# GNN message passing with a segment maximum: the edge table spread by exclusive-or and float minimum

## The chip, the cores and the metric

One core of one Trainium2 chip runs the whole program. The metric is device microseconds (us) from launch to end of that program; lower is better. A core has five engines with instruction streams of their own: TensorE (PE in the profile, with its weight loads as PEld), VectorE (DVE), ScalarE (ACT), GpSimd (POOL) and SyncE (SP). In this kernel SP only issues transfers, and GpSimd issues the indirect ones, which gather rows by a list of indices. What an engine waits for is told to it by semaphores.

## The reference

One layer of a graph network over N = 6,250 nodes with D = 256 values each and E = 100,000 edges, which come sorted by their target `dst`:

```python
def reference(x, src, dst, theta_w, theta_b, phi_w, phi_b):
    x_src, x_dst = x[src], x[dst]
    e = relu((x_dst - x_src) @ theta_w.T + theta_b + x_src @ phi_w.T + phi_b)
    out = segment_max(e, dst, num_segments=N)
    out = where(isfinite(out), out, 0.0)
    return layernorm(x + out, axis=-1)          # over D, eps 1e-5
```

All values are float32. Since the maximum over the edges of a node commutes with adding what belongs to that node alone, what has to be computed per node is max over its edges of `b_rows[src]`, where `b_rows = x @ (phi_w - theta_w).T` is one table of 6,250 rows. The term of the target, the bias, the relu, the sum with x and the normalisation come at the end, once for each node.

## The kernel before, in words

**The table of rows.** x is read in 12 transfers (`x_q`), transposed on PE, copied by ACT and multiplied with the weights (L758); the result goes to `b_rows` in DRAM. The weights are the difference of the two given matrices, transposed on PE and copied by DVE (L739).

**Part 1, the first 1,130 nodes.** Their edges lie in 128 partitions of 146 columns. GpSimd gathers one column of 128 rows at a time (L512, one instruction for each column; `gather`), into a ring of six tiles `g` of eight columns. The first 48 columns are gathered from x itself and multiplied on PE; behind each of these gathers two instructions on a small tile (L488, `pause`) space them out. The other 98 columns come from `b_rows`. DVE folds a column into the running maximum of its partition (L688 in `run`, 146 of them, "steps"), SP stores eight steps at once (L696, `maxima`), and at the end one row per node is fetched back.

**Part 2, the other 5,120 nodes,** 40 tiles of 128. Here the edges are found on the chip. Each partition owns 40 nodes and looks at a window of 800 edges (`dst_w` and `src_w`, gathered from DRAM, L653). `fill_table` (L928 to L985) spreads them into a table of 36 ranks for each of 40 nodes (1,440 words in a partition): an edge's word is its distance to its place in the table times `WORD`, plus a code of its source, and ten steps move a word by 512, 256, ... 1 where its distance is at least that. A step is three DVE operations (L966, L969, L972), which go between two tables in turn. An empty place is a zero. At the end `padded` holds the codes as int16 by [rank, node], with a large code where there is no edge (L979).

A code says in which "slot" a source lies: b_rows is cut into 17 slots of 383 rows, three blocks of 128 with one row to spare, and the code is slot times 512 plus the row in the slot. `choice` (L995 to L1021) picks, for two slots at a time, at most one edge for each node and slot, by an exclusive-or of `padded` and a minimum over 24 ranks; `wanted` (L1023 to L1030) transposes the result `chosen` on PE and stores it as rows of words (`chosen_rows`). Then 85 "parts" follow, one for each slot and 1,024 nodes (`slot_part`, L1060): SP loads the words to all partitions (`want`, L1065), ACT makes a one-hot matrix from them in two operations for a block (L1071, L1072; from the list stage's end on, DVE makes one block of three, L1069), and PE multiplies it with the slot's rows, in two terms of reduced precision (L1057 by ACT, L1058 by DVE, from `raw`): 24 matmuls (L1079). DVE folds the result into `acc` (L1090; for slot 0 ACT copies it). `raw` is one tile for all slots. Its spare row needs a very small number, which a memset (L1034) puts there once; SP loads the rest for each slot.

**The list.** Edges that no slot took go to a list (`list_pieces`, L1171 to L1240): DVE marks and counts them, closes the gaps in 11 steps, and stores the words; 232 gathers from `b_rows` (`list_src`) follow, with running maxima of their own (again L688).

**The order.** Each engine's order is fixed when the program is built, by a scheduler that goes by the engines' modelled times and by who needs what; where an order is wanted it is written as a dependence without a semaphore (`behind_in_order`). So is GpSimd's (`in_turn`), and a step of part 1 behind the gathers of the next group. The top of the part around the change is

```python
fill_table()
paced[0] = 0
for s0 in range(0, NS, BATCH_S):
    choice(s0)
    wanted(s0)
    next_group_1(1)     # eight gathers, eight steps of the group before, one slot_part
```

and behind it come `list_pieces` and the rest of part 1, with two parts to a group, then the list's groups with the other parts, then the end: x + relu(...), the sums for the normalisation, and four stores. If an edge list doesn't fit the assumptions (counted in `bad`), a general path at the very end does the work anew; it is not taken here.

Of the kernel before, what the change touches and what calls it, by code (L numbers as in the profile page):

```python
# [41 lines left out]
I32 = mybir.dt.int32  # L42
# [5 lines left out]
ALU = mybir.AluOpType  # L48
# [4 lines left out]
P = 128  # L53
# [8 lines left out]
WINDOW = 800  # L62
R = 36
ROWS = 127
KB = 3
SLOT = 512
# [2 lines left out]
PAUSE = 160  # L69
CHOICE_R = 24  # L70
X_AFTER = 6
WORD = 8720
TABLE_BITS = 10
SLOT_BITS = 9
P_BITS = 7
# [3 lines left out]
OWN_LIST = 288  # L79
LIST_CHUNK = 232  # L80
LIST_GROUPS = (LIST + STEPS - 1) // STEPS
BACK = 34
# [3 lines left out]
FAR = 1000000.0  # L86
GENERAL_STEPS = 17
LOWEST = -1.0e30
ABSENT = 1 << 14
MAGIC = 12582912.0  # L90
PARTS = 2

# [335 lines left out]
def gnn_kernel(ctx: ExitStack, tc: tile.TileContext, x, src, dst, theta_w, theta_b, phi_w, phi_b, out):  # L428
    nc = tc.nc
    N, D = x.shape  # L430
# [9 lines left out]
    TR = TILES * R  # L440
    SLOT_ROWS = (KB - 1) * P + ROWS
    NS = -(-N // SLOT_ROWS)
    CW = 1024
    CHUNKS = OWN // CW
    EDGES = 1 << SORT_BITS
    NONE_1 = P * T1
    assert D == 2 * P and LEFT1 > 0 and OWN % CW == 0 and TILES < 64 and P * T1 < E and WINDOW < E
    assert (P - 1) * T + 1 < E <= P * T and N < ID_MASK and P * T <= EDGES and E + 8 * P <= EDGES
    assert SLOT * NS < min(ABSENT, WORD) and WORD << TABLE_BITS <= 1 << 24 and SLOT == 1 << SLOT_BITS and P == 1 << P_BITS and SLOT_ROWS < SLOT and KB == 3 and ROWS == P - 1 and WINDOW <= 8 * P and OWN_LIST * P < 1 << 20
    BATCH_S = 2  # L450
    assert STEPS == 1 << STEPS_BITS and LIST <= 2 * P and 3 * BATCH_S * CHOICE_R * TILES // 2 + TR <= 6 * WINDOW and LIST_CHUNK + 1 == LIST and LIST_CHUNK % STEPS == 0 and 3 * (BACK + LIST_CHUNK) <= WINDOW and BACK == R - 2 and CARRY_GROUPS * STEPS >= BACK and BACK + LIST_CHUNK <= OWN_LIST and R == 36 and CHOICE_R == 24 and OWN_LIST <= 512 and 1024 + OWN_LIST <= TR < 1024 + 512

# [34 lines left out]
    def iota(t, step, base, per_partition):  # L487
        return nc.gpsimd.iota(  # L488
            t,
            pattern=[[step, t.shape[1]]],  # L490
            base=base,
            channel_multiplier=per_partition,
            allow_small_or_imprecise_dtypes=True,
        )
# [7 lines left out]
    def behind_in_order(one, name, reason):  # L502
        after = mybir.DependencyInfo(mybir.DependencyClass.NoSync, mybir.DependencyReason.DATA)
        tc.add_manual_dep(one.ins, name, after, reason=reason)
# [80 lines left out]
    first_node = const.tile([P, 1], FP, name="first_node")  # L585
# [336 lines left out]
    def floor_of(to, value, divisor):  # L922
        nc.vector.tensor_scalar(
            to, value, 1.0 / divisor, -(divisor - 1) / (2.0 * divisor), op0=ALU.mult, op1=ALU.add
        )
        nc.vector.tensor_scalar(to, to, MAGIC, MAGIC, op0=ALU.add, op1=ALU.subtract)

    def fill_table():  # L928


        W = WINDOW
        local, w_1, w_2 = (wide[:, i * W : (i + 1) * W] for i in range(3))
        source, w_3 = work_2[:, :W], work_1[:, TR - W :]
        iota(w_3, 1, TR - W + 1, 0)
        nc.vector.memset(words[:, : TR - W], 0.0)
        nc.vector.memset(work_1[:, : TR - W], 0.0)
        nc.vector.tensor_scalar(local, dst_w, first_node, None, op0=ALU.subtract)

        nc.vector.tensor_scalar(bad[:, 1:2], local[:, 0:1], 0.0, None, op0=ALU.is_ge)
        far = W - (TR - (1 << TABLE_BITS)) - 1  # L940
        nc.vector.tensor_scalar(bad[:, 4:5], local[:, far : far + 1], 0.0, None, op0=ALU.is_lt)
        valid = w_1
        nc.vector.tensor_scalar(valid, local, 0.0, None, op0=ALU.is_ge)
        same = w_2
        nc.vector.memset(same[:, 0:1], 0.0)
        nc.vector.tensor_tensor(same[:, 1:], local[:, 1:], local[:, : W - 1], op=ALU.is_equal)
        nc.vector.tensor_tensor_scan(same, same, valid, 0.0, ALU.mult, ALU.add)
        nc.vector.tensor_scalar(
            source, same, float(R), None, op0=ALU.is_gt, op1=ALU.add, accum_out=bad[:, 5:6]
        )  # L950
        nc.vector.scalar_tensor_tensor(w_3, local, float(-R), w_3, op0=ALU.mult, op1=ALU.add)
        distance = w_3
        nc.vector.tensor_tensor(distance, w_3, same, op=ALU.subtract)
        nc.vector.tensor_copy(source, src_w)
        slot = local
        floor_of(slot, source, SLOT_ROWS)
        nc.vector.tensor_scalar(source, source, 1.0, None, op0=ALU.add)
        nc.vector.scalar_tensor_tensor(source, slot, float(SLOT - SLOT_ROWS), source, op0=ALU.mult, op1=ALU.add)
        nc.vector.scalar_tensor_tensor(source, distance, float(WORD), source, op0=ALU.mult, op1=ALU.add)
        nc.vector.tensor_tensor(words[:, TR - W :], source, valid, op=ALU.mult)  # L960
        now, then, going = words, work_1, work_2
        for i in reversed(range(TABLE_BITS)):
            step = 1 << i
            first = TR - W if step >= TR - W - step else 0
            a = max(first, step)
            nc.vector.tensor_scalar(  # L966
                going[:, a:], now[:, a:], float(-step * WORD), 0.0, op0=ALU.add, op1=ALU.max
            )
            nc.vector.scalar_tensor_tensor(  # L969
                then[:, first:], now[:, first:], float(step * WORD), now[:, first:], op0=ALU.is_lt, op1=ALU.mult  # L970
            )
            nc.vector.tensor_tensor(  # L972
                then[:, a - step : TR - step], then[:, a - step : TR - step], going[:, a:], op=ALU.add
            )
            now, then = then, now
        assert now is words
        nc.vector.tensor_scalar(work_1, words, 0.0, ABSENT + 1.0, op0=ALU.is_equal, op1=ALU.mult)
        nc.vector.scalar_tensor_tensor(
            padded.rearrange(by_rank, r=R),  # L979
            words.rearrange("p (j r) -> p r j", r=R),  # L980
            -1.0,
            work_1.rearrange("p (j r) -> p r j", r=R),
            op0=ALU.add,
            op1=ALU.add,
        )  # L985

# [44 lines left out]


    raw = slots.tile([P, KB, D], FP, name="raw", bufs=1)
    nc.vector.memset(raw, LOWEST)  # L1034
    terms_of = {}
    dve_hots = [0]

# [132 lines left out]

    def list_pieces():  # L1171
        left_over = wide_i16(3 * BATCH_S * CHOICE_R * TILES // 2, [P, TR])
        nc.vector.scalar_tensor_tensor(left_over, padded, float(ABSENT), unused, op0=ALU.is_lt, op1=ALU.mult)
        valid, count = work_1, work_2
        nc.vector.tensor_copy(valid.rearrange(by_node, r=R), left_over.rearrange("p (r j) -> p j r", r=R))
        nc.vector.tensor_tensor_scan(count, valid, valid, 0.0, ALU.add, ALU.max)  # L1176
# [15 lines left out]
            op=ALU.add,  # L1192
# [31 lines left out]
        for i, to in enumerate((second, third)):  # L1224
            nc.vector.tensor_scalar(mask, edge, ends[:, i + 1 : i + 2], None, op0=ALU.is_ge)
            nc.vector.copy_predicated(list_edges, mask, to)
        key, slot = (t.bitcast(I32)[:, :LIST_CHUNK] for t in (wide[:, WINDOW : 2 * WINDOW], count))
        nc.vector.tensor_scalar(key, list_edges[:, BACK:], (1 << 14) - 1, None, op0=ALU.bitwise_and)
        nc.vector.tensor_scalar(key, key, -1, 0, op0=ALU.add, op1=ALU.max)
        nc.vector.tensor_scalar(slot, key, SLOT_BITS, None, op0=ALU.logical_shift_right)  # L1230
        nc.vector.scalar_tensor_tensor(list_src, slot, SLOT_ROWS - SLOT, key, op0=ALU.mult, op1=ALU.add)
        nc.vector.tensor_scalar(list_src, list_src, N - 1, None, op0=ALU.min)
        list_node = list_edges
        nc.vector.tensor_scalar(list_node, list_edges, 14, (1 << 13) - 1, op0=ALU.logical_shift_right, op1=ALU.bitwise_and)
# [262 lines left out]
```

## Time and profile before

| | |
|---|---|
| median of 3 runs | 744.11 us (743.1 to 745.2) |
| the profiled execution's own time | 744.23 us |
| its span (first to last instruction) | 742.4 us |
| PE busy | 655.6 us, 88% of the span |
| DVE busy | 636.6 us, 86% |
| POOL busy | 515.8 us, 69% |
| ACT busy | 507.7 us, 68% |
| bytes moved | 164.83 MB, a mean of 222 GB/s |
| mean clock granted to TensorE | 0.969 of full speed |
| L1079 on PE, the parts' matmuls | 463.6 us in 1,960 recorded instructions, 397 ns each |
| L512 on POOL, gathers of part 1 from b_rows | 130.4 us in 98, 1,330 ns each |
| L688 on DVE, running maxima of both kinds | 180.3 us in 376, 479 ns each |

Busy times are shares of one profiled execution. Matmuls are pipelined, so a busy PE need not be at its peak. A "q" behind an engine's name (SPq, POOLq) marks its transfers. The chain that ended last is by lines 45% L1079; by engines PE 49%, DVE 8%, POOL 7%, DMA 6%, ACT 6%.

### The profile page before, as it was taken

To read this page: it belongs to the slowest core of one execution; us is meant where nothing else is said; L and a number is where in the kernel's file an instruction comes from. 1 tells how busy PE (TensorE), PEld (TensorE's weight loads), DVE (VectorE), ACT (ScalarE), POOL (GpSimd) and SP (SyncE) were. 2 spreads that over 40 slices of the span, in tenths; PEclk is the share of its full clock that TensorE was granted. 3 is DMA by queue.
4 is the path that set the end of the run, shared out by engine and by line. 5 is a ranking of instruction groups with operands and counts; after the bars stand their busy time and mean duration, and the time that the engine had idled before them with its cause. 6 is when DMAs were issued, how large, how long until landed. Compare 5 with 4: busy or idle time off the path is not lost.

```text
span 742.4 us, 10003 instructions
## 1 busy us (share of the span) xinstructions
PE 655.6 (88%) x3018; PEld 540.4 (73%) x3018; DVE 636.6 (86%) x1213; ACT 507.7 (68%) x714; POOL 515.8 (69%) x561
## 2 busy tenths in 40 slices
PE   0599998998875998899999999999999999789943
PEld 0388787886664866688888888888888888579943
DVE  6499999999987988498979888889888989968874
ACT  0144446969995797688778777877877776037882
POOL 7598987888987777777777777777767364037710
PEclk9999999999997899999999999999999999999986
DMA  7476756576477678988787878778867676336652
GB/s 219 135 254 207 274 192 221 167 255 205 139 228 231 215 215 300 300 295 271 235 264 221 283 250 248 242 240 284 269 209 244 186 255 208 137 107 192 206 200 76
DMA packets 56470, 164.83 MB, mean 222 GB/s; under 512 B 11899, under 2 KB 19860, under 8 KB 49332
## 3 DMA queue, kind: packets, MB, share of 16 engines
q1 hardware_dynamic: 32920, 98.76, 38.5%
q0 software_dynamic: 20944, 57.62, 27.3%
q10 hardware_dynamic: 2540, 7.69, 2.8%
q8 instruction: 27, 0.44, 0.3%
q14 instruction: 39, 0.32, 0.1%
HBM read 101.08 MB, written 63.74 MB: 222 GB/s over the span
## 4 chain that ended last, share of the span: by engine, by line
PE 49%; DVE 8%; POOL 7%; DMA 6%; ACT 6%; issue 4%; SPq 0%; DVEq 0%; ACTq 0%; POOLq 0%
PE ps_f L1079 45%; POOL g L512 6%; DMA g<-b_rows,src 4%; DMA want<-chosen_rows 2%; ACT x_f L1348 2%; ACT squares L1333 2%; PE ps_e L1303 2%; DVE acc L1090 2%; DVE g L688 1%; ACT x_t L1298 1%; DVE g L1314 1%; DVE x_f L1318 1%; PE ps_e L1296 1%; DVE work L1176 0%; POOL dst_w L512 0%
## 5 line engine op out<-in xcount | busy, mean ns | idle before, releaser
L1079 PE MATMUL ps_f<-hot,terms 128*128 128x512 f32 x1960 | 463.6, 397 | 30.7 <-DVE acc L1090 15.2
L1079 PEld LDWEIGHTS ps_f<-hot,terms 128*128 128x128 f32 x1960 | 371.9, 191 | 118.5 <-DVE acc L1090 18.5
L512 POOL DMA_INDIRECT g<-b_rows,list_src x232 | 233.2, 1005 | 84.6 <-issue 61.1
L1071 ACT ACTIVATE hot<-want,minus_row 128x1024 fp32r<-128x1024 f16 x179 | 197.4, 1146 | 82.6 <-PE ps_f L1079 72.6
L1090 DVE TENSOR_TENSOR acc<-acc,ps_f 128x1024 f32<-128x1024 f32 x160 | 193.4, 1215 | 30.5 <-PE ps_f L1079 29.6
L688 DVE SCALAR_TENSOR_TENSOR g<-g,caps 128x256 f32<-128x256 f32 x376 | 180.3, 479 | 15.2 <-DMA g<-b_rows,src 11.7
L1072 ACT ACTIVATE hot<-hot 128x1024 fp32r<-128x1024 f32 x179 | 179.5, 1047 | 0.0
L512 POOL DMA_INDIRECT g<-b_rows,src x98 | 130.4, 1330 | 30.0 <-issue 25.9
L758 PE MATMUL ps_b<-weights,x_t 128*128 128x256 f32 x388 | 92.4, 393 | 5.1 <-ACT x_t L748 4.5
L758 PEld LDWEIGHTS ps_b<-weights,x_t 128*128 128x128 f32 x388 | 74.0, 196 | 19.1 <-ACT x_t L748 9.3
L512 POOL DMA_INDIRECT g<-maxima,place x49 | 47.1, 962 | 54.6 <-DVE g L1315 29.2
L512 POOL DMA_INDIRECT g<-in_x_dram,src x48 | 62.5, 1302 | 11.6 <-issue 6.6
L1069 DVE TENSOR_SCALAR hot<-want,row_id 128x1024 fp32r<-128x1024 f16 x66 | 50.4, 766 | 6.7 <-DMA want<-chosen_rows 6.7
L1303 PE MATMUL ps_e<-weights,x_t 128*128 128x256 f32 x192 | 49.4, 386 | 0.2 <-ACT x_t L1298 0.2
L1303 PEld LDWEIGHTS ps_e<-weights,x_t 128*128 128x128 f32 x192 | 33.6, 195 | 3.8 <-ACT x_t L1298 0.5
L761 ACT COPY b_sb<-ps_b 128x512 f32<-128x512 f32 (+1 forms) x25 | 14.5, 578 | 29.1 <-PE ps_b L758 29.1
L1298 ACT COPY x_t<-ps_e 128x512 f32<-128x512 f32 x24 | 13.7, 575 | 29.6 <-PE ps_e L1296 29.6
L488 POOL IOTA pause<- 128x160 f32 x102 | 29.9, 293 | 3.4
L748 ACT COPY x_t<-ps_xt 128x512 f32<-128x512 f32 (+1 forms) x49 | 26.4, 594 | 6.1 <-PE ps_xt L746 5.9
L1333 ACT ACTIVATE squares<-x_f,r 128x256 bf16<-128x256 f32 x49 | 24.3, 500 | 7.7 <-DVE r L1330 7.7
L1348 ACT ACTIVATE x_f<-x_f,r 128x256 f32<-128x256 f32 x41 | 21.5, 591 | 9.2 <-DVE r L1340 9.1
L761 ACT COPY g<-ps_b 128x512 f32<-128x512 f32 x24 | 14.1, 589 | 17.8 <-PE ps_b L758 16.7
(267 smaller groups left out, 500.2 us busy)
## 6 DMA issues: line engine op xcount, KB each, us to landing
maxima<-g SPq DMA_DIRECT2D x47, 1024.0 KB
want<-chosen_rows SPq DMA_DIRECT2D x85, 256.0 KB
x_q<-in_x_dram SPq DMA_DIRECT2D x12, 512.0 KB
b_rows<-b_sb ACTq DMA_DIRECT2D x12, 512.0 KB
raw<-b_rows SPq DMA_DIRECT2D x16, 256.0 KB
x_f<-in_x_dram SPq DMA_DIRECT2D x4, 1024.0 KB
out_dram<-x_f SPq DMA_DIRECT2D x4, 1024.0 KB
g<-b_rows,list_src POOLq DMA_INDIRECT x232, 3.9
```

The costliest lines, as they stand in the source:

```text
L488: return nc.gpsimd.iota(t, pattern=[[step, t.shape[1]]], base=base, channel_multiplier=per_partition, allow_small_or_imprecise_dtypes=True,)
L512: in_turn(nc.gpsimd.indirect_dma_start(out=out, out_offset=out_offset, in_=in_, in_offset=in_offset))
L688: one = nc.vector.scalar_tensor_tensor(g[:, k, :], last[part], caps[:, t : t + 1], g[:, k, :], op0=ALU.min, op1=ALU.max)
L758: nc.tensor.matmul(ps[:, h, :], x_t[:, h, k, :], weights[:, k, 0, :], start=(k == 0), stop=(k == KC - 1))
L1069: nc.vector.tensor_scalar(hot[:, b, :], want, row_id[:, b : b + 1], None, op0=ALU.is_equal)
L1071: nc.scalar.activation(hot[:, b, :], want, AF.Abs, bias=minus_row[:, b : b + 1], scale=1.0)
L1072: nc.scalar.activation(hot[:, b, :], hot[:, b, :].bitcast(FP), AF.Relu, bias=1.0, scale=-1.0)
L1079: nc.tensor.matmul(ps[:, w : w + 512], terms[:, part, b, h * P : (h + 1) * P], hot[:, b, w : w + 512], start=(i == 0), stop=(i == n - 1),)
L1090: latest_part[0] = nc.vector.tensor_tensor(to, to, ps, op=ALU.max).ins.name
L1303: nc.tensor.matmul(a[:, i, :], x_t[:, 2 * i + c, :], weights[:, c, 1, :], start=(c == 0), stop=False)
L1333: nc.scalar.activation(squares, x_f[:, k, :], AF.Square, bias=mean[:, k : k + 1], scale=1.0, accum_out=var[:, k : k + 1])
L1348: nc.scalar.activation(x_f[:, k, :], x_f[:, k, :], AF.Identity, bias=mean[:, k : k + 1], scale=inv[:, k : k + 1])
```

## The change

`WORD` becomes 2^13, so that the source number itself (13 bits) is the lower part of a word and the distance (10 bits) the upper, 23 bits in all. 2^23 is added to each word: as a float32 it then has these 23 bits as its mantissa, and an exclusive-or on the bits of one distance bit raises the word where that bit was clear and lowers it where it was set. A step takes the exclusive-or with its bit (int32, into `work_2`) and the float minimum of what was there and what comes from further on, in place in `words`; empty places hold 2^100 and give way to any word. So a step has two operations, not three. A word that has moved on leaves a copy behind, whose distance is not zero; the minimum with `WORD - 1` behind the steps turns these copies, and the empty places, into one code beyond all slots. Edges ahead of the window's first node get a large negative `valid` (by `FAR_OFF`); the 0.5 added to `local` keeps it off zero, and the 18 (R // 2) added to `w_3` takes that out of the product with 36 again.

The slot codes, before made for the window's edges ahead of the steps, are made behind them for the whole table (`floor_of`, two operations, and one that writes `padded`). The list takes the source number from the word by an "and" where it went back from the code in four operations. The memset of `work_1` is gone. The memset of `raw` is moved from behind `wanted` into `fill_table` and ordered behind the instruction that writes the words.

```diff
--- before.py
+++ after.py
@@ -69,7 +69,7 @@
 PAUSE = 160
 CHOICE_R = 24
 X_AFTER = 6
-WORD = 8720
+WORD = 1 << 13
 TABLE_BITS = 10
 SLOT_BITS = 9
 P_BITS = 7
@@ -86,7 +86,8 @@
 FAR = 1000000.0
 GENERAL_STEPS = 17
 LOWEST = -1.0e30
-ABSENT = 1 << 14
+EMPTY = 2.0**100
+FAR_OFF = 2.0**30
 MAGIC = 12582912.0
 PARTS = 2
 
@@ -444,9 +445,10 @@
+    slot_code = lambda i: i + i // SLOT_ROWS * (SLOT - SLOT_ROWS)
...
@@ -931,16 +933,15 @@
         W = WINDOW
         local, w_1, w_2 = (wide[:, i * W : (i + 1) * W] for i in range(3))
         source, w_3 = work_2[:, :W], work_1[:, TR - W :]
-        iota(w_3, 1, TR - W + 1, 0)
-        nc.vector.memset(words[:, : TR - W], 0.0)
-        nc.vector.memset(work_1[:, : TR - W], 0.0)
-        nc.vector.tensor_scalar(local, dst_w, first_node, None, op0=ALU.subtract)
+        iota(w_3, 1, TR - W + 1 + R // 2, 0)
+        nc.vector.memset(words[:, : TR - W], EMPTY)
+        nc.vector.tensor_scalar(local, dst_w, first_node, 0.5, op0=ALU.subtract, op1=ALU.add)
 
         nc.vector.tensor_scalar(bad[:, 1:2], local[:, 0:1], 0.0, None, op0=ALU.is_ge)
         far = W - (TR - (1 << TABLE_BITS)) - 1
         nc.vector.tensor_scalar(bad[:, 4:5], local[:, far : far + 1], 0.0, None, op0=ALU.is_lt)
         valid = w_1
-        nc.vector.tensor_scalar(valid, local, 0.0, None, op0=ALU.is_ge)
+        nc.vector.tensor_scalar(valid, local, FAR_OFF, 1.0, op0=ALU.mult, op1=ALU.min)
         same = w_2
         nc.vector.memset(same[:, 0:1], 0.0)
         nc.vector.tensor_tensor(same[:, 1:], local[:, 1:], local[:, : W - 1], op=ALU.is_equal)
@@ -951,36 +952,28 @@
         nc.vector.scalar_tensor_tensor(w_3, local, float(-R), w_3, op0=ALU.mult, op1=ALU.add)
         distance = w_3
         nc.vector.tensor_tensor(distance, w_3, same, op=ALU.subtract)
-        nc.vector.tensor_copy(source, src_w)
-        slot = local
-        floor_of(slot, source, SLOT_ROWS)
-        nc.vector.tensor_scalar(source, source, 1.0, None, op0=ALU.add)
-        nc.vector.scalar_tensor_tensor(source, slot, float(SLOT - SLOT_ROWS), source, op0=ALU.mult, op1=ALU.add)
-        nc.vector.scalar_tensor_tensor(source, distance, float(WORD), source, op0=ALU.mult, op1=ALU.add)
-        nc.vector.tensor_tensor(words[:, TR - W :], source, valid, op=ALU.mult)
-        now, then, going = words, work_1, work_2
+        nc.vector.tensor_scalar(source, src_w, float(1 << 23), None, op0=ALU.add)
+        one = nc.vector.scalar_tensor_tensor(
+            words[:, TR - W :], distance, float(WORD), source, op0=ALU.mult, op1=ALU.add
+        )
+        behind_in_order(nc.vector.memset(raw, LOWEST), one.ins.name, "edge table ahead of a slot's rows")
+        going = work_2
         for i in reversed(range(TABLE_BITS)):
             step = 1 << i
-            first = TR - W if step >= TR - W - step else 0
-            a = max(first, step)
+            a = max(TR - W if step >= TR - W - step else 0, step)
             nc.vector.tensor_scalar(
-                going[:, a:], now[:, a:], float(-step * WORD), 0.0, op0=ALU.add, op1=ALU.max
+                going.bitcast(I32)[:, a:], words.bitcast(I32)[:, a:], step * WORD, None, op0=ALU.bitwise_xor
             )
-            nc.vector.scalar_tensor_tensor(
-                then[:, first:], now[:, first:], float(step * WORD), now[:, first:], op0=ALU.is_lt, op1=ALU.mult
-            )
-            nc.vector.tensor_tensor(
-                then[:, a - step : TR - step], then[:, a - step : TR - step], going[:, a:], op=ALU.add
-            )
-            now, then = then, now
-        assert now is words
-        nc.vector.tensor_scalar(work_1, words, 0.0, ABSENT + 1.0, op0=ALU.is_equal, op1=ALU.mult)
+            nc.vector.tensor_tensor(words[:, a - step : TR - step], words[:, a - step : TR - step], going[:, a:], op=ALU.min)
+        nc.vector.tensor_scalar(words, words, float(1 << 23), float(WORD - 1), op0=ALU.subtract, op1=ALU.min)
+        slot = work_1
+        floor_of(slot, words, SLOT_ROWS)
         nc.vector.scalar_tensor_tensor(
             padded.rearrange(by_rank, r=R),
+            slot.rearrange("p (j r) -> p r j", r=R),
+            float(SLOT - SLOT_ROWS),
             words.rearrange("p (j r) -> p r j", r=R),
-            -1.0,
-            work_1.rearrange("p (j r) -> p r j", r=R),
-            op0=ALU.add,
+            op0=ALU.mult,
             op1=ALU.add,
         )
 
@@ -1031,7 +1024,6 @@
 
 
     raw = slots.tile([P, KB, D], FP, name="raw", bufs=1)
-    nc.vector.memset(raw, LOWEST)
     terms_of = {}
     dve_hots = [0]
 
@@ -1170,7 +1162,7 @@
 
     def list_pieces():
         left_over = wide_i16(3 * BATCH_S * CHOICE_R * TILES // 2, [P, TR])
-        nc.vector.scalar_tensor_tensor(left_over, padded, float(ABSENT), unused, op0=ALU.is_lt, op1=ALU.mult)
+        nc.vector.scalar_tensor_tensor(left_over, padded, float(SLOT * NS), unused, op0=ALU.is_lt, op1=ALU.mult)
         valid, count = work_1, work_2
         nc.vector.tensor_copy(valid.rearrange(by_node, r=R), left_over.rearrange("p (r j) -> p j r", r=R))
         nc.vector.tensor_tensor_scan(count, valid, valid, 0.0, ALU.add, ALU.max)
@@ -1224,11 +1216,7 @@
         for i, to in enumerate((second, third)):
             nc.vector.tensor_scalar(mask, edge, ends[:, i + 1 : i + 2], None, op0=ALU.is_ge)
             nc.vector.copy_predicated(list_edges, mask, to)
-        key, slot = (t.bitcast(I32)[:, :LIST_CHUNK] for t in (wide[:, WINDOW : 2 * WINDOW], count))
-        nc.vector.tensor_scalar(key, list_edges[:, BACK:], (1 << 14) - 1, None, op0=ALU.bitwise_and)
-        nc.vector.tensor_scalar(key, key, -1, 0, op0=ALU.add, op1=ALU.max)
-        nc.vector.tensor_scalar(slot, key, SLOT_BITS, None, op0=ALU.logical_shift_right)
-        nc.vector.scalar_tensor_tensor(list_src, slot, SLOT_ROWS - SLOT, key, op0=ALU.mult, op1=ALU.add)
+        nc.vector.tensor_scalar(list_src, list_edges[:, BACK:], WORD - 1, None, op0=ALU.bitwise_and)
         nc.vector.tensor_scalar(list_src, list_src, N - 1, None, op0=ALU.min)
         list_node = list_edges
         nc.vector.tensor_scalar(list_node, list_edges, 14, (1 << 13) - 1, op0=ALU.logical_shift_right, op1=ALU.bitwise_and)
```

The hunk around line 444 holds besides only bounds that the program asserts when it is built; `slot_code` is used there alone.

2 lines of the change are left out of this document (1 added, 1 removed).

## The prediction

> **What bounds the kernel now.** I read the busy time by stretches first, then the chain, then the timelines of VectorE (DVE), GpSimd (POOL), SyncE (SP) and ScalarE (ACT) around the table. In the table by stretches the columns are the stretch, its length, busy time of PE, PEld, DVE, ACT and POOL with counts, TensorE's clock, DMA share and GB/s.
>
> ```profile
> 30.00:95.00 65.00, 61.59 (x320) 53.02 (x320) 63.75 (x80) 29.03 (x55) 56.64 (x85) 1.00 0.69 227
> 155.00:240.00 85.00, 66.62 (x261) 50.21 (x260) 78.19 (x147) 74.67 (x101) 71.12 (x48) 0.91 0.65 207
> 240.00:312.00 72.00, 64.95 (x266) 50.27 (x265) 55.65 (x120) 55.13 (x57) 55.69 (x57) 0.96 0.82 259
> 312.00:622.00 310.00, 309.96 (x1368) 256.48 (x1369) 274.93 (x400) 242.48 (x242) 219.06 (x218) 1.00 0.78 247
> ```
>
> From 312 to 622 PE is never idle: what the change does to the 312 us ahead of that shifts the end one for one, and nothing later can give it back. Up to 152 PE is full too, with b_rows and the x groups. Between lie the first 21 "parts" (one slot and 1,024 nodes, 24 matmuls each, L1079), and there PE waits. The edge table is DVE's work at 33 to 93 us, where DVE is 98% busy, but nobody else waits for it then: PE has its own work until 152. So the table is on the path only through what DVE does later. What that is, four timelines show (start, us, engine, line, operation, idle time before it and its releaser):
>
> ```profile
> 30.63 0.70 DVE L1034 MEMSET raw<- 128x768 f32 x1 [3.33 <-POOLq L653]
> 47.37 0.98 DVE L969 SCALAR_TENSOR_TENSOR work<-words 128x800 f32<-128x800 f32 x1
> 48.38 0.99 DVE L972 TENSOR_TENSOR work<-work,work 128x800 f32<-128x800 f32 x1
> 242.13 0.48 DVE L688 SCALAR_TENSOR_TENSOR g<-g,caps 128x256 f32<-128x256 f32 x1 [2.54 <-DMA g<-b_rows,src]
> ```
> ```profile
> 181.62 2.16 POOL L512 DMA_INDIRECT g<-b_rows,src  x1 [0.30 <-issue]
> 184.08 9.06 POOL L512 DMA_INDIRECT g<-b_rows,src  x1 [0.30 <-issue]
> ...
> 217.44 0.95 POOL L512 DMA_INDIRECT g<-b_rows,src  x1 [0.30 <-issue]
> ```
> ```profile
> 227.69 7.54 SPq L696 DMA_DIRECT2D maxima<-g  x2
> 235.33 0.37 SPq L1065 DMA_DIRECT2D want<-chosen_rows  x1
> ```
> ```profile
> 231.45 1.15 ACT L1071 ACTIVATE hot<-want,minus_row 128x1024 fp32r<-128x1024 f16 x1 [4.79 <-PE ps_f L1079]
> 245.92 0.84 ACT L1057 CAST terms<-raw 128x768 fp32r<-128x768 f32 x1 [7.46 <-DVE g L688]
> 301.62 2.19 ACT L1071 ACTIVATE hot<-want,minus_row 128x1024 fp32r<-128x1024 f16 x2 [3.21 <-DMA want<-chosen_rows]
> ```
>
> From 217 us on DVE itself waits for gathered rows (the bracket in its line at 242.13). GpSimd issues one gather per running-maximum step, never stops from 23 to 285 us, and needs 0.95 + 0.30 us for one when DVE is quiet, but up to 9.06 us in DVE's list stage. SP stands on a store of eight such steps (L696) and issues the next word load (L1065) right behind it; ACT makes the one-hot words from that (5.97 us for the three blocks of a part: two L1071 take 2.08 from start to start, two L1072 1.90). So in 217 to 312 the order is gathers, DVE steps, store, word load, ACT, PE.
>
> **The change, part by part.** *The ten steps.* They start at 46.87 and end at 88.93; seven running-maximum steps at 0.39 lie among them, so 39.3 us are the table's. The ten L969 go (0.98 + 9 x 1.65 = 15.8). The ten L966 (8.7 in all) become exclusive-ors on int32: nearest row the int32 shift L1195, 0.90 for 1,440 elements, like L966's 0.91; the ten L972 (15.5) become minima at the same size. Every operation now depends on the one before it (0.04 gap, as between L969 and L972 above, instead of a 0.08 overlap): 8.7 + 15.5 + 20 x 0.04 = 25.0. Saved: 14.3. *Ahead of the loop* L923, L926, L957, L958 and L960 go (0.68 + 0.57 + 0.68 + 0.98 + 0.99 = 3.9); the cast (0.56) becomes an addition, at 0.92 by L937, which also reads int32: 3.5 saved; raw's memset comes in, 0.70 lost. *Behind it* one 0.91 stays as the subtraction and two floors of 0.91 are added: 1.9 lost. The early memset L936 (0.59) ran at 14.25, where DVE has gaps: nothing. *Raw's memset at the head* blocked DVE until 30.63, and L739 (the weights that PE waits 3.6 us for) behind it. Without it the next in order is L937, whose dst_w was issued at 23.49 and landed 3.8 us later, at 27.3: everything behind starts about 2.7 us earlier (1.9 if the landing counts from the gather's end). With four running-maximum steps that fall behind the table (1.6), padded is done at 92.6 - 14.3 - 3.5 + 0.7 + 1.9 - 2.7 - 1.6 = 73, some 19.5 us earlier. In the list stage three key operations of 0.27 to 0.39 go, two of them hidden: nothing.
>
> *PE's start.* PE gets the weights 2.7 us earlier, but the new order puts the first transposition of `chosen` (L1027) and a place matmul in front of the matmuls that began at 80.13. PE is there at 77.4; `chosen` comes 5.9 us behind padded, less 0.87 for L1058 that moves out, plus four steps of 0.40: 79.6. PE waits 2.2 and has two small matmuls more (0.4). L1079 starts at 153 as before, give or take 1.5.
>
> *The gathers.* x gathers (paced) took 2.3 us each beside the table and 1.87 beside the choices: from 34.1 to 73 at the first and then at the second they end at 114, not 118.6. Beside choices with steps between them, 1.45 each (29.5 in 42.8 us). DVE reaches the list stage (L1173, before 162.7) at 131: 57.9 us behind padded, 70.1 less 28 steps and an idle 0.96. That stage is some 48 us of long operations in both, and 19 gathers took 50.4 us there, 2.65 each. After that 1.29 (21 in 27.1 us from 214.89). So: gather 60 at 131, 78 at 179.5, 81 at 184, 135 at 253.5; three list gathers 4.4; the last, 145, at 270, landing 2.4 later; the last store at 274 instead of 293.5. A gain of about 20 us. The Trainium skill, page "SBUF — State Buffer", section "Who interferes with whom", has a rule for such pairs: whoever issues first holds the shared port pair for that whole instruction, the other one waits. The 9.06 us gather sat through more than eight VectorE instructions, so here the trace does not agree; what the rule would make of the sum is rival 1.
>
> *The orders.* The built order takes it back. The first accumulation (L1090) stands behind 89 steps instead of 83, the ninth behind 121 instead of 111, the seventeenth behind 145 (all) instead of 127. On SP the word load of part 10 stands behind store 12 instead of 10, of part 14 behind 15 instead of 13, of part 17 behind 18, the last, instead of 15. So part 17's words are issued not at 264.3 but at 275. They follow two stores and two x_f loads, as did the load that went out at 293.94 and landed at 301.62: 7.7 us, 282.7 (13.4 for the load behind it, issued at 295.46). Then ACT makes parts 17 to 19: 3 x 5.97, 300.6; PE ends part 19 2.5 later, 303.1, and parts 20 to 22, where DVE takes a block of three, at 24 x 0.227 each: 319.4. Before, 508 matmuls (21 parts and 4) had gone by 312.04, and part 22 ended 20 x 0.227 later, at 316.6. So +2.8. The profiled execution took 744.23 (span 742.4 and 1.8 outside; the median of the runs is 744.11): 744.2 + 2.8 = 747.0.
>
> **The rivals.** *1, faster: gathers are freed more than I take.* If a gather waits for one VectorE operation at most (0.95 + 1.86), the list stage goes at the rate of its gathers under 2.81 us: mean 1.58, with 0.30 1.88. 48 us then hold 25.5 instead of 18, everything behind is 7.5 x 1.29 = 9.7 us earlier: 737. That is what the page's rule says too. For it: without the 9.06 us gather alone the rate is 2.3. Against it: four more gathers of 3.4 us and over in that stage. *2, much slower: the words meet the x_f loads.* If each load of parts 17 to 19 takes the 13.4 us that the one of 295.46 took, part 17 starts 5.7 us later, and a 1 MB x_f load lies ahead of each of the next two (some 4 us at 259 GB/s, half of it hidden): 747 + 5.7 + 4 = 757. A list stage at the 3.05 of its first 35 us gives 3 of these too. It decides once a word load takes over 12 us, two parts. *3, nothing:* the 19.5 us end in DVE waits and no chain moves: 744.
>
> **How the numbers follow.** About 0.3%, 2.2 us, is what a measurement of this kernel can tell from no change. The forecast, 743 to 752, has 0.55: of it 0.36 slower, 0.14 within, 0.05 faster. Rival 1 has 0.24 (733 to 741, faster), rival 2 0.16 (slower), rival 3 0.05 (within). Faster 0.29, same 0.19, slower 0.52. Eight in ten lie between 735, where the lower third of rival 1 is left out, and 758.
>
> **What would show it.** Right: padded written near 73 us; gathers of 0.95 us from about 185 on; the last store of part 1 near 274; word loads 14 and 17 issued right behind stores 15 and 18, ACT idle in front of parts 14 to 17 for `want`, and PE still full from part 20 on at about the same time as before. Wrong: gathers at under 2 us through the list stage, part 17's words on the chip before 272, or PE's full stretch starting more than 5 us away from 315. A matmul start on L1079 before 150 would show the weights' 2.7 us kept.

## The result, and the profile after

The changed kernel takes 768.63 us (median of 4 runs, 763.26 to 772.01) beside 744.65 us before: a ratio of 1.031, 95% interval 1.023 to 1.039. The profiled execution took 771.72 us, its span 769.8. It is slower, as forecast, but by 24 us and not by 3, and outside the range of 735 to 758. Medians are of all runs; ratios leave out slow runs, those over 1.5% above the fastest of the same kernel. The profiled execution is one of the two longer ones of the four.

First the busy time by stretches of the changed kernel, columns as in the prediction:

```profile
155.00:240.00 85.00, 50.98 (x194) 37.89 (x192) 57.04 (x103) 53.32 (x75) 70.52 (x50) 0.80 0.61 202
240.00:312.00 72.00, 52.78 (x195) 41.26 (x196) 48.02 (x133) 47.62 (x49) 55.48 (x61) 0.85 0.78 253
312.00:622.00 310.00, 310.00 (x1365) 256.58 (x1364) 263.97 (x373) 248.17 (x250) 206.63 (x207) 1.00 0.75 236
```

PE is still full from 312 on. The loss lies between 155 and 312: 50.98 + 52.78 = 103.8 us of PE's time instead of 131.6, 27.8 us less, which is the growth of the span (27.4). By 312.04 us, 381 matmuls of L1071 (L1079 before) had begun, instead of 509; at 0.227 us each the 128 that are missing are 29 us. The granted clock goes with PE's idle time: 0.80 and 0.85 here, 0.91 and 0.96 in the same stretches before the change, 1.00 in the full stretch behind. Whether the lower clock costs time of its own is not separated here.

What the engines waited for from 155 to 312 (engine, line, whom it waited for, us in total, times, longest):

```profile
PE ps_f L1071 <- DVE acc L1082: 40.9, 6, 20.7
DVE g L690 <- DMA g<-b_rows,src: 33.5, 20, 4.5
ACT hot L1063 <- DMA want<-chosen_rows: 33.4, 6, 10.8
```

And before the change, in the same stretch:

```profile
PE ps_f L1079 <- DVE acc L1090: 15.2, 7, 4.5
...
DVE g L688 <- DMA g<-b_rows,src: 11.7, 7, 2.5
...
ACT hot L1071 <- DMA want<-chosen_rows: 6.4, 2, 3.2
```

An accumulation (VectorE's maximum of a result into `acc`) frees the buffer that PE writes next. PE's waits for accumulations grew by 25.7 us, its other large wait, for one-hot matrices, by 2.7 (10.4 against 7.7). One of these waits is 20.7 us long; at 218 us, behind it, 59 matmuls are missing, and 112 at 296 us, so later accumulations cost as much again. VectorE's timeline shows what the first one stood behind:

```profile
188.28 1.52 DVE L690 SCALAR_TENSOR_TENSOR g<-g,caps 128x256 f32<-128x256 f32 x3
193.08 1.53 DVE L690 SCALAR_TENSOR_TENSOR g<-g,caps 128x256 f32<-128x256 f32 x3 [3.28 <-DMA g<-b_rows,src]
...
210.46 3.10 DVE L690 SCALAR_TENSOR_TENSOR g<-g,caps 128x256 f32<-128x256 f32 x6 [4.50 <-DMA g<-b_rows,src]
...
216.09 1.21 DVE L1082 TENSOR_TENSOR acc<-acc,ps_f 128x1024 f32<-128x1024 f32 x1
```

with PE's first matmul behind it, and a gather that held up all gathers behind it:

```profile
217.36 4.88 PE L1071 MATMUL ps_f<-hot,terms 128*128 128x512 f32 x11 [20.70 <-DVE acc L1082]
```
```profile
174.84 0.99 POOL L514 DMA_INDIRECT g<-b_rows,src  x1 [0.30 <-issue]
176.13 13.04 POOL L514 DMA_INDIRECT g<-b_rows,src  x1 [0.30 <-issue]
189.47 1.14 POOL L514 DMA_INDIRECT g<-b_rows,src  x1 [0.30 <-issue]
```

VectorE has finished the list stage at 188 and has little to do from there but running-maximum steps (L690), each behind its gathered row. The first accumulation (L1082) stands behind 89 of them, and comes at 216.1; PE, which ended its last matmul at 196.7, stands until then. Before the change the first accumulation came at 197.8, behind 83 steps and four of the list's eleven shifts (L1207); now all eleven stand ahead of it. The rows of before:

```profile
194.51 1.79 DVE L1207 COPY_PREDICATED work<-words,work 128x1432 int32<-128x1432 int32 x1
...
197.79 1.21 DVE L1090 TENSOR_TENSOR acc<-acc,ps_f 128x1024 f32<-128x1024 f32 x1
...
200.85 1.78 DVE L1207 COPY_PREDICATED work<-words,work 128x1424 int32<-128x1424 int32 x1
```

### The profile page after: what moved, and what is told of

The parts are those of the page before. It is cut to its first block, busy times and chain, and to the rows that moved or that the text cites. A ratio compares the mean times of both kernels' runs of the same rounds, so it can differ in the third digit from the quotient of the medians.

```text
span 769.8 us, 9986 instructions
## 1 busy us (share of the span) xinstructions
PE 655.6 (85%) x3018; PEld 543.2 (71%) x3018; DVE 622.9 (81%) x1196; ACT 507.4 (66%) x714; POOL 518.7 (67%) x561
## 4 chain that ended last, share of the span: by engine, by line
PE 46%; POOL 11%; DMA 8%; DVE 8%; ACT 5%; issue 4%; SPq 0%; DVEq 0%; POOLq 0%; ACTq 0%
PE ps_f L1071 43%; POOL g L514 10%; DMA g<-b_rows,src 5%; ACT x_f L1336 2%; ACT squares L1321 2%; DVE acc L1082 2%; PE ps_e L1291 2%; DMA want<-chosen_rows 2%; DVE g L690 2%; ACT x_t L1286 1%; DVE g L1302 1%; DMA maxima<-g 1%; PE ps_e L1284 1%; DVE x_f L1306 0%; DVE hot L1061 0%
## 5 line engine op out<-in xcount | busy, mean ns | idle before, releaser
L1071 PE MATMUL ps_f<-hot,terms 128*128 128x512 f32 x1960 | 466.0, 399 | 56.7 <-DVE acc L1082 40.9
L1071 PEld LDWEIGHTS ps_f<-hot,terms 128*128 128x128 f32 x1960 | 375.9, 193 | 142.9 <-DVE acc L1082 43.4
L1082 DVE TENSOR_TENSOR acc<-acc,ps_f 128x1024 f32<-128x1024 f32 x160 | 193.4, 1216 | 56.3 <-PE ps_f L1071 55.3
L690 DVE SCALAR_TENSOR_TENSOR g<-g,caps 128x256 f32<-128x256 f32 x376 | 180.5, 480 | 37.0 <-DMA g<-b_rows,src 33.5
L760 PE MATMUL ps_b<-weights,x_t 128*128 128x256 f32 x388 | 89.9, 386 | 3.6 <-ACT x_t L750 3.1
L514 POOL DMA_INDIRECT g<-maxima,place x49 | 47.2, 964 | 52.7 <-DVE g L1303 27.4
L514 POOL DMA_INDIRECT g<-in_x_dram,src x48 | 67.4, 1404 | 11.4 <-issue 7.1
L763 ACT COPY g<-ps_b 128x512 f32<-128x512 f32 x24 | 14.1, 587 | 21.9 <-PE ps_b L760 21.9
```

The costliest lines, as they stand in the source:

```text
L514: in_turn(nc.gpsimd.indirect_dma_start(out=out, out_offset=out_offset, in_=in_, in_offset=in_offset))
L690: one = nc.vector.scalar_tensor_tensor(g[:, k, :], last[part], caps[:, t : t + 1], g[:, k, :], op0=ALU.min, op1=ALU.max)
L760: nc.tensor.matmul(ps[:, h, :], x_t[:, h, k, :], weights[:, k, 0, :], start=(k == 0), stop=(k == KC - 1))
L1071: nc.tensor.matmul(ps[:, w : w + 512], terms[:, part, b, h * P : (h + 1) * P], hot[:, b, w : w + 512], start=(i == 0), stop=(i == n - 1),)
L1082: latest_part[0] = nc.vector.tensor_tensor(to, to, ps, op=ALU.max).ins.name
```

## The experiments

The theories as the expectations name them. *GATHERS*, later worded as *LATE ROWS*: VectorE reaches the list stage 28 us earlier, but GpSimd's gathers do not come earlier; the built order puts accumulations behind steps (and later a merge) whose rows are late. *ORDERS*: the number of steps and stores ahead of an accumulation or a word load costs, whatever the rows do. *WORD LOADS*: the prediction's own path, loads (L1065 before) behind stores on SyncE. *MEMSET*: raw's memset, moved into the table. Ratios are to the kernel before on the same chip. The edits are cut to the lines that matter; left out are those that collect the steps, shifts and accumulations in lists.

### Undo one part: raw's memset at its old place (after_raw_head)

```diff
-        behind_in_order(nc.vector.memset(raw, LOWEST), one.ins.name, "edge table ahead of a slot's rows")
...
     raw = slots.tile([P, KB, D], FP, name="raw", bufs=1)
+    nc.vector.memset(raw, LOWEST)
```

> The changed kernel with raw's memset back at its old place, ahead of the table and without the written order. VectorE's order of accumulations and SyncE's order stay as in the changed kernel. Theory GATHERS (VectorE reaches the list stage some 28 us earlier, GpSimd's gathers do not come earlier, so steps, and the accumulations behind them, wait for rows): VectorE starts the table 2 to 3 us later, all else stays, 763 to 772 us. Theory ORDERS (the built order alone, stores ahead of word loads and steps ahead of accumulations, takes the time): the same, 763 to 772. Theory MEMSET (the move is what costs): back to 743 to 750.

Measured: 766.01 us, ratio 1.030 (1.021 to 1.040). The move of the memset is not the cause. The first operation on `dst_w` began at 33.5 us here and at 31.8 in the changed kernel (33.4 before), so without the memset ahead of it it starts 1.7 us earlier, where the prediction has 2.7; but padded was written at 73.9 here and at 75.1 there, so none of it was left at the table's end.

This run also tells how much of the profile above belongs to one execution. Its orders are those of the changed kernel, but its gathers run some 7 us ahead (the 135th begins at 263.4 instead of 270.6), and PE's longest wait is 12.3 us and not 20.7. PE still waits 34.6 us for accumulations from 155 to 312, and the time is within 3 us.

### Fill the saved time with work that nobody reads (after_filler)

```diff
             nc.vector.tensor_tensor(words[:, a - step : TR - step], words[:, a - step : TR - step], going[:, a:], op=ALU.min)
+            nc.vector.tensor_tensor(work_1, words, going, op=ALU.min)
```

> The changed kernel with one more minimum of 1,440 words in each of the ten steps (into work_1, which nobody reads), 10 x 1.66 = 16.6 us more VectorE work, so that padded comes near 92 us as before the change. The built order of accumulations (83, 88, 92, 100, 111 steps ahead) and of word loads is then that of the kernel before. GATHERS: the time of before, 742 to 750 us, with PE's 21 us wait near 200 us gone. ORDERS: also 742 to 750, since the order is back. MEMSET: raw's memset is still in the table, so 760 or more.

Measured: 746.13 us, ratio 1.000 (0.996 to 1.004). Sixteen us of useless work take 22 us off the time. Padded comes at 91.5, the first accumulation at 196.8 behind 83 steps; the stretches are those of before:

```profile
155.00:240.00 85.00, 63.25 (x253) 47.62 (x251) 75.43 (x140) 73.24 (x100) 72.33 (x44) 0.92 0.61 196
240.00:312.00 72.00, 65.74 (x260) 51.64 (x260) 55.98 (x123) 53.76 (x56) 54.44 (x55) 0.91 0.80 252
```

So the new operations as such do not make the kernel slower: what costs is that VectorE is done earlier, and the order that the scheduler builds from that.

### Earlier rows, the order unchanged (after_paced0)

```diff
-    paced = [2]
+    paced = [0]
```

> The changed kernel without the two pause instructions of 0.3 us behind each of the 48 gathers from x; the built order on VectorE and SyncE stays exactly that of the changed kernel (first accumulation behind 89 steps and all eleven shifts of the list). GATHERS: the gathers run 20 to 28 us earlier at the list stage, the first accumulation comes near 197 us instead of 216, PE's 21 us wait is mostly gone: 743 to 754 us. ORDERS: the order is the same, so 760 to 772.

Measured: 756.71 us, ratio 1.015 (1.006 to 1.023). The last part-1 gathers come 15 us earlier than in the changed kernel, the first accumulation at 201.6 instead of 216.1. PE waits 28.7 us for accumulations instead of 40.9. With the order of the changed kernel kept, earlier rows win about half of the loss back. The median lies between what GATHERS (743 to 754) and ORDERS (760 to 772) expected; the interval, some 751 to 763 us, reaches into both. That the rows matter is seen at the first accumulation, which stands behind the same 89 steps.

### No steps among the list's operations (after_no_mix)

```diff
+    behind_in_order(steps_1[26], shifts[-1], "the list's words first")
```

`steps_1` holds the steps of part 1, `shifts` the list's copies (L1199).

> The changed kernel with the running-maximum steps from the 27th on ordered behind the last shift of the list stage, so that VectorE has one dependent chain there and not two interleaved ones. GATHERS, with the holding of a gather by VectorE's gapless stream as its cause: no gather over 4 us between 135 and 175 us (13.04 us before), list stage done near 172 us, gathers some 15 us earlier at the 83rd, first accumulation near 197 us, 745 to 756 us. If a gather is held by the kind of VectorE operation and not by the lack of gaps, gathers stay at 3 us and over in the list stage and the time is 762 to 775. ORDERS: the first accumulation stands behind 77 steps instead of 89, word loads behind the same stores: 755 to 768.

Measured: 768.96 us, ratio 1.033 (1.025 to 1.040), outside what GATHERS gave, and just above what ORDERS did; it lies in the range of the third alternative, whose condition (gathers of 3 us and over) did not come. The longest gather in the list stage is 3.52 us and not 13.04 (mean 2.32 of 14, instead of 3.11 of 16), the first accumulation comes at 202.2, and PE's long wait there is gone. That the edit shortened the gathers is not shown, though: in the next run the steps alternate with the list's operations as in the changed kernel, and there the longest is 3.79 and the mean 2.22. The edit also had a price. The ring of row tiles filled up while the steps stood back, and GpSimd stood 12.74 us for the first of them. And a second wait of PE has come, at another operation that waits for GpSimd:

```profile
270.98 0.46 DVE L1221 COPY_PREDICATED dst_w<-words,dst_w 128x266 int32<-128x266 int32 x1 [11.64 <-DMA dst_w<-list_words,run_start]
```

This is the list's merge of words that three gathers bring; in GpSimd's written order they stand behind 136 of part 1's 146, and VectorE got there too early. PE stood 14.1 us for the accumulation behind it.

### The steps at their old places (after_old_order)

```diff
+    for i, n in enumerate((83, 88, 92, 100, 111, 116, 119, 123, 127)):
+        behind_in_order(steps_1[n], accs[2 * i + 1], "VectorE's order")
```

`accs` holds the accumulations, two for each part.

> The changed kernel with its short table, and nine running-maximum steps ordered behind the accumulations that stood ahead of them before the change (first pair of accumulations behind 83 steps, then 88, 92, 100, 111, 116, 118, 122, 127 instead of 89, 99, 108, 117, 121, 127, 132, 140, 145); all eleven list shifts still stand ahead of the first pair. Theory LATE ROWS (both matter: how many steps stand ahead of an accumulation, and when the rows of these steps arrive): the 83rd step came at 211 us in the changed kernel, so the first pair only moves from 216 to 211 us, later pairs by 10 to 15 us: 752 to 760 us. Theory ORDERS (the number of steps alone): the time of before, 743 to 750.

Measured: 770.26 us, ratio 1.037 (1.021 to 1.053), against both theories. The accumulations came within some 4 us of before the change up to the ninth (234.7 us; 235.1 before), and then the same merge held everything:

```profile
DVE dst_w L1222 <- DMA dst_w<-list_words,run_start: 22.6, 1, 22.6
```

Before the change the merge stood behind ten pairs of accumulations; the scheduler had now put it behind five. PE's longest wait follows from it; the second row is this run's last word load ahead of that wait, the third the same load before the change:

```profile
268.69 1.65 PE L1074 MATMUL ps_f<-hot,terms 128*128 128x512 f32 x3 [21.31 <-DVE acc L1085]
240.01 0.34 SPq L1060 DMA_DIRECT2D want<-chosen_rows  x1
240.60 0.38 SPq L1065 DMA_DIRECT2D want<-chosen_rows  x1
```

So VectorE's order alone can cost PE 21 us: this word load was no later than before the change.

### The steps and the merge at their old places (old_order_list_2)

```diff
+    for i, n in enumerate((83, 88, 92, 100, 111, 116, 119, 123, 127, 127, 132, 138, 143)):
+        behind_in_order(steps_1[n], accs[2 * i + 1], "VectorE's order")
+    behind_in_order(first_list[0], accs[19], "VectorE's order")
```

`first_list[0]` is the first merge.

> The changed kernel with the steps in their old places behind the accumulations (83, 88, 92, 100, 111, 116, 118, 123, 127, 127, 132, 137, 143 steps ahead) and the list's first merge of gathered words behind the tenth pair of accumulations, where it stood before the change. With the steps alone in their old places this merge stood behind six pairs and VectorE waited 22.6 us at it. LATE ROWS (whatever GpSimd delivers late must not stand ahead of an accumulation): the 22.6 us go, accumulations 10 to 18 come at 240 to 272 us as before the change, 741 to 751 us. If the loss sits in the word loads, which stand behind 11 to 16 stores here, 757 or more.

Measured: 747.27 us, ratio 0.999 (0.995 to 1.004). That is the whole loss, won back by an order written for VectorE alone, with the short table, with raw's memset where the change put it, with all eleven shifts ahead of the first accumulation, and with a gather of 8.96 us still held in the list stage. PE's waits for accumulations fall from 40.9 to 10.6 us, and ScalarE's for words from 33.4 to 13.5:

```profile
PE ps_f L1074 <- DVE acc L1085: 10.6, 2, 6.2
...
ACT hot L1066 <- DMA want<-chosen_rows: 13.5, 5, 4.6
```

It does not part VectorE's order from the word loads. The edit is on VectorE, but SyncE's built order came back with it: part 17's words are issued behind store 15 again, as before the change (18 in the changed kernel). The three rows are of the kernel before, the changed kernel and this run:

```profile
264.32 0.32 SPq L1065 DMA_DIRECT2D want<-chosen_rows  x1
296.41 0.41 SPq L1057 DMA_DIRECT2D want<-chosen_rows  x1
264.99 0.32 SPq L1060 DMA_DIRECT2D want<-chosen_rows  x1
```

### Word loads off SyncE, the order of accumulations held (pinned_want_act_2)

```diff
-        nc.sync.dma_start(want, flat(chosen_rows,
+        nc.scalar.dma_start(want, flat(chosen_rows,
...
+        behind_in_order(acc_ops[2 * i], steps_1[n - 1].ins.name, "VectorE's order")
```

and the steps behind the accumulations, both ways, at the changed kernel's places.

> The changed kernel with the order of steps and accumulations on VectorE pinned as it is there (89, 99, 108, 117, 121, 127, 132, 140 steps ahead), and the word loads issued from ScalarE's queue, so that none of them stands behind a store of maxima. LATE ROWS: the accumulations still wait for the rows of the steps ahead of them, 760 to 773 us, and ScalarE's 33 us of waiting for words turns into waiting for PE. WORD LOADS (the prediction's mechanism, loads behind stores on SyncE): with the loads free of the stores 743 to 753 us.

Measured: 783.07 us, ratio 1.051 (1.045 to 1.057). It lies above what either theory expected. Freeing the loads of the stores wins nothing by itself: ScalarE's waiting for words falls from 33.4 to 10.9 us, and its waiting for PE rises from 11.8 to 36.8, while PE goes on waiting for accumulations.

```profile
ACT hot L1066 <- PE ps_f L1074: 36.8, 5, 12.6
...
PE ps_f L1074 <- DVE acc L1085: 30.1, 5, 13.6
```

From 155 to 312 PE works 106.1 us, 2 more than in the changed kernel; why the rest of this kernel is slower still was not followed. The test is not a clean one: the loads now stand in ScalarE's order, and part 17's went out at 307.6 us, later than in the changed kernel; and the merge, which was not held in its place, stands behind one pair of accumulations fewer, and VectorE waits 10.6 us at it (5.2 in the changed kernel).

### An even order (after_even_order)

```diff
+    for i, n in enumerate((73, 77, 82, 86, 91, 95, 99, 104, 108, 113, 117, 121, 126, 130, 135, 139, 143)):
+        behind_in_order(steps_1[n], accs[2 * i + 1], "VectorE's order")
+    behind_in_order(first_list[0], accs[29], "VectorE's order")
```

> The changed kernel with an even order on VectorE: pair j of accumulations stands behind 73 + 4.4 j steps, and the list's first merge of gathered words behind pair 14. 5.5 us is what PE needs for a part and 1.25 us a gather, so 4.4 gathers fall to a part. LATE ROWS: the 73rd step came at 196 us, the first pair comes at 197 us, nothing on VectorE waits over 5 us for rows ahead of an accumulation, PE's 21 us wait is gone: 733 to 746 us. ORDERS, by stores ahead of word loads (now 9 to 14 for parts 8 to 17, from 11 to 19): the same range. If the loss came from VectorE's or GpSimd's work as such, 760 or more.

Measured: 731.69 us, ratio 0.983 (0.970 to 0.997): 37 us off the changed kernel, a little below the expected 733 to 746, and faster than the kernel before. A gather of 13.02 us is still there, at 176.7; the first accumulation comes at 194.6 all the same, behind 73 steps.

```profile
155.00:240.00 85.00, 75.55 (x321) 57.47 (x320) 76.22 (x166) 82.14 (x104) 70.38 (x49) 1.00 0.66 214
240.00:312.00 72.00, 65.34 (x267) 50.35 (x266) 58.17 (x102) 60.01 (x63) 53.78 (x56) 0.95 0.85 275
```

No wait of PE for an accumulation is left. PE works 140.9 us from 155 to 312, 9 more than in the kernel before and 37 more than in the changed one.

### The even order without the pauses (after_even_paced0, and beside it on one chip before_even_paced0_2 and after_even_paced0_2)

The edits are the two above together, in the changed kernel and in the kernel before.

> The same even order, and no pause instructions behind the gathers from x (48 x 0.6 us on GpSimd). LATE ROWS: the 73rd row lies there 10 us earlier, the waits that are left shrink: 728 to 742 us, and 3 to 10 us less than with the even order alone. If with the even order nobody waits for rows any more, the same time as with it alone, within 3 us.

> The kernel before the change, with its long table, with the even order (pair j of accumulations behind 73 + 4.4 j steps, the list's merge behind pair 14) and without the pauses. LATE ROWS: 727 to 737 us. If VectorE's time in the table is not on the path even with the right order, within 4 us of the changed kernel with both in this call; if the shorter table pays once nothing waits for rows, 5 us or more above it.

> The changed kernel with the even order and without the pauses, once more, beside the kernel before with the same two edits: 724 to 733 us, 0.970 to 0.985 of the kernel before. If the table's time is off the path, no faster than the kernel before with both edits, within 4 us; if it pays now, 5 us or more faster.

Measured: 728.60 us (0.979; 0.965 to 0.994) and, once more, 729.51 us (0.977; 0.973 to 0.981); the kernel before with the same edits 737.18 us (0.988; 0.983 to 0.992). The last two are from one call, and their intervals don't overlap: with the right order the change is worth 7.7 us. VectorE's time in the table had not been off the path for good. The fastest version of this study is the changed kernel with both edits, 2.3% under the kernel before. What the pauses add to the even order, 3.1 us, is not shown: the single runs with them (730.7 to 734.6) and without (727.3 to 732.6) overlap.

### The pauses alone, before the change (before_paced0)

> The kernel before the change without the pause instructions; its built orders stay as they were. LATE ROWS: VectorE waited 11.7 us for rows between 155 and 312 us, of which some 5 us stand ahead of accumulations, and its long list stage holds gathers as before: 736 to 745 us. If the pauses keep gathers out of the way of x's loads or of the table, 747 to 760.

Measured: 735.89 us, ratio 0.987 (0.967 to 1.006). It lies at the lower edge of the expected range of 736 to 745, and the interval takes in no change.

### Four experiments on another chip (after_old_order_list, after_pinned_want_act, before_even_order, before_even_paced0)

On one chip the kernel before took 925 us. The traces of these four runs have 17 to 25 us in which no engine worked, in pieces of 1 to 6 us (1 to 2 us in all in the traces of before and after), which does not explain the 180 us; what does is not known. The steps and the merge at their old places gave a ratio of 1.017 (1.007 to 1.026) there; the word loads off SyncE gave 1.029 (1.021 to 1.037); the kernel before with the even order and without the pauses 0.993 (0.988 to 0.998). These three are the ones repeated above. The first does not agree with its repetition (0.999 on the other chip), and the argument rests on the repetition; the changed kernel itself was not run on this chip. The kernel before with the even order alone (944.08 us; 914 to 946) gave no ratio and was not repeated, so what that order is worth there by itself stays open.

## Why the prediction was wrong, step by step

**The table: right.** The ten steps took 25.4 us (43.26 to 68.62; forecast 25.0), padded was written at 75.1 (73), the list stage reached at 134.3 (131). L1071 started at 151.0 (153, give or take 1.5). The weights did not reach PE 2.7 us earlier, however: PE waited for VectorE's copy of them until 33.0 us (31.9 before), and lost less time on the way to 151.

**The gathers: the term that was mis-sized.** The prediction has the last gather of part 1 begin at 270 us (284.6 before) and the last store go out at 274 (293.5 before), a gain of about 20 us. The gather began at 288.8 and the store went out at 293.4: no gain at all. There were two shortfalls. The last gather from x ended at 123.5 instead of 114: one gather that met the end of the table and the first choices took 7.23 us, where the prediction goes on at 1.87 us each. At the list stage 55 gathers were done, not 60. And in the list stage a gather took 3.11 us in the mean, with 0.30 us between two, and one took 13.04; the prediction has 2.65 with the 0.30. So the 78th began at 197.2 (forecast 179.5) and the 135th at 270.6 (253.5). In after_raw_head the first shortfall was mostly absent (117.9 us, 59 gathers done) and the second there in part (2.73 us in the mean; the 78th at 189.1). Rates read from one stage of before were carried over to a VectorE stream that the change had moved. Rival 1, that the gathers would be freed more than taken, is the wrong way round.

**The orders: the accumulations, the term that was put at nothing.** This is the step that failed. The prediction read the built order rightly (89 steps for 83, 121 for 111, word load 17 behind the last store) and let it end in the word loads. It names the accumulations' places and gives them no price. In the trace PE's waits for them grew from 15.2 to 40.9 us. The path by word load 17 came as described, and later: the words were issued at 296.4 instead of 275. Put into the prediction's own sum, 21.4 us more than 747.0 give 768, but that agreement is luck: when these words were issued PE was already 112 of its 128 matmuls behind (343 begun by 296 us, 455 before). What share the earlier word loads have stays open, since in the runs that won the loss back they had moved back too. That accumulations alone can cost nearly as much is shown by after_old_order, with PE 21.3 us behind a merge and word loads no later than before.

**The list stage in that order** was not read either: before, seven of the eleven shifts stood behind the first accumulation, now none. The loss does not hang on that, since in old_order_list_2 all eleven stand ahead too and the time is that of before.

**Rival 2** (757) had the direction and a size nearer to the truth. Part 17's words were used 11.6 us after they were issued (296.4 to 308.0), near its 13.4, but most of the loss lay ahead of them, so its mechanism is not what made it.

## What to carry to other kernels

An operation that becomes faster on an engine with a fixed order changes that order: the scheduler fills the time it sees with whatever its model says is ready, here steps whose rows a slower engine had not yet brought. When a cut off the path makes a kernel slower, pad the cut with useless work: if the time comes back, it is the order and not the new operations. Then write the order by hand at the rate at which the slow producer really delivers (here 24 x 0.227 = 5.5 us for a part and 0.95 + 0.30 = 1.25 us for a gather: 4.4 gathers to a part). Count for every instruction that frees another engine's buffer what stands ahead of it and which of that waits for a third engine, and do it for every such producer: one merge left out took back all that the steps had gained.

## What the runs showed of the hardware that was not expected

A gather issued by GpSimd can be held far longer than one VectorE instruction. It took 0.95 us when VectorE was quiet, and 13.04 us beside 25 VectorE instructions, two chains taking turns, each instruction starting before the one ahead had ended. By the Trainium skill, page "SBUF — State Buffer", section "Who interferes with whom", GpSimd shares a port pair with VectorE in its two-port modes, and whoever issues first holds the pair for that instruction while the other one waits; here the wait went on through many, and no run shows in which mode they ran.

How long a gather is held does not follow from that stream alone. In the changed kernel and in six of its variants 38 steps lay among the list's operations with no gap between instructions, and the longest gather of the stage was 13.04 us (after), 13.02 (after_even_order), 8.96 (old_order_list_2), 8.92 (after_paced0), 6.18 (after_raw_head) and 3.79 (after_old_order and after_even_paced0). The one of 13.04 ended 0.42 us after the first gap in VectorE's stream (0.036 us, at 188.75), the one of 7.23 ended 0.84 us after such a gap; but those of 9.06 (before) and 8.96 (old_order_list_2) ended with no gap near them. What lets a gather in stays open.
